# The seven half tiles of a mixture of experts spread among the whole ones, beside a linear recurrence

## The chip, the core and the metric

The kernel runs on one core of a Trainium2 chip. The metric is the device time of one execution in microseconds. The engines are TensorE (PE in the profile, PEld for its weight loads), VectorE (DVE), ScalarE (ACT), GpSimd (POOL) and SyncE (SP), which here only issues DMAs. All data is float32.

## The reference

Tokens x of shape (8, 512, 256) are normalised to xn. One branch is a recurrent attention with 16 heads of 16, the other a top-2 mixture of 8 experts (256 to 1024 to 256). The result is x + s * g.

```python
q, k = silu(x @ Wq), l2_norm(silu(x @ Wk)); v = x @ Wv
a = k * gamma[..., None] * exp(gk)
def step(S, inp):
    S = S * exp(gkt)[..., None]
    sab = einsum('bhk,bhkv->bhv', at, S)
    S = S + kt[..., None] * (sab[..., None, :] + vt[..., None, :])
    return S, einsum('bhk,bhkv->bhv', qt, S)
...
for e in range(num_experts):
    h = gelu(xf @ W1[e] + b1[e]); y = h @ W2[e] + b2[e]
    out = out + cw[:, e:e + 1] * y
...
xn = layernorm(x)
s = attn(xn); g = silu(layernorm(ffn(xn)) * gamma + beta)
return x + s * g
```

## The kernel before

**The recurrence.** The 512 steps are cut into 8 segments of 64, and these into chunks of 16 or 8 steps in turn (CS), 48 chunks in all. For each chunk there are two sets of small matmuls: `by_state` (L901), which multiplies the state, and `by_keys` (L966), which makes the addition to it. VectorE adds the values between the two (`add_v`, L932) and renews the state after them (`renew`, L978). This is a chain: each chunk needs the state of the one before. VectorE also solves each segment ahead of its chunks (`fine`, `solve`: L710 to L823) and works out its outputs after them (`output`, L1029, L1038). Each segment's data moves through DRAM in several steps, on the SP queue: raw (L657), fq (L787), kt (L823), R (L1009, L1012), the o store (L1042), KT for each chunk (L882) and the values vz (L871). `attend` then gates, normalises and projects a segment. For the last two segments its final part waits until the experts are done.

**The experts.** Rows are sorted by expert into blocks of 128. There are NXW = 32 whole tiles of two blocks and NXH = 7 half tiles of one, at numbers 32 to 38, which take the odd blocks of experts. Each tile is processed in the same way whatever expert it has:

- its two weights, 1 MB each, are loaded into one of two buffers each, on SP (`load_weights`, L1084 and L1086), always for every tile, and its rows are gathered on POOL (`load_rows`, L1072);
- `turn` transposes the rows (L1094, copied at L1098);
- the first layer (L1125) runs over the tile's 256 or 128 rows with 1024 columns, in four steps of two Gelus (L1133);
- the second layer (L1150) runs for each block of 128 rows, ScalarE scales the result (L1158), and an indirect DMA on POOL adds it to y_dram (`add_to_sums`, L1102).

Weights are asked for one tile ahead and rows two, both at the first of the four steps of a tile. Inside tiles there are also sixteen copies of 256 KB from x to out (L1139), one in every second tile, to which the results are added in the end.

**The order of the work.** Everything is written as generators that yield planned costs in units of about a microsecond: a step of the first layer is 1.9, a turn 0.9, a block of the second layer 3.9, so a whole tile 16.3 and a half tile 12.4. `stretch` walks the 48 chunks. Between the steps of a chunk it spends a share of the experts' remaining cost (`per_chunk`), so that about four chunks' worth (AFTER) is left behind the chain. Each engine then works in the order in which it got its instructions, but for a scheduler's small moves. After the last tile `fetch_sums` (L1282) reads y_dram back, and `finish` does the last norms, the product with the attention and the addition to out.

```python
beside_cost = experts_cost + (NTB - 2) * 7 * 1.8 + 16 * 0.8 + 8 * 8.6 + 10
...
per_chunk = max(0.0, beside_cost - beside.spent) / (chunks + AFTER)
```

Of the kernel before, what the change touches and what calls it, by code (L numbers as in the profile page):

```python
# [30 lines left out]
def recurrent_attn_moe_kernel(  # L31
# [29 lines left out]
    NF = DFF // P  # L61
    NTB = T // NB
# [6 lines left out]
    NXW, NXH = 2 * NT * P // TS, E - 1  # L69
    NX = NXW + NXH  # L70
# [8 lines left out]
    def bank(name):  # L79
        return ps_p.tile([P, 512], F32, tag="ps", name=name)  # L80
# [61 lines left out]
    for i in range(2):  # L142
        t = sp.tile([P, GC, 2 * D], F32, name=f"vz{i}", bufs=1)
# [5 lines left out]
    def rows_of(ap, s, bb):  # L149

        return ap.rearrange("(c bb) t d -> bb t c d", bb=2)[bb, s * NB : (s + 1) * NB]
# [913 lines left out]
    def pieces(t):  # L1065

        return range(2 * t, 2 * t + 2) if t < NXW else (NXW + t,)

    def load_rows(t):
        xs = cp[0].tile([P, TS // P, D], F32, name="xs", bufs=3)  # L1070
        for n, r in enumerate(pieces(t)):
            nc.gpsimd.indirect_dma_start(  # L1072
                out=xs[:, n],
                out_offset=None,
                in_=xn_dram[:, :],
                in_offset=bass.IndirectOffsetOnAxis(ap=source[:, r : r + 1], axis=0),
            )
        return xs

    def experts(mp):  # L1080
        def load_weights(t):
            e = nc.sync.value_load(owner[0:1, t : t + 1], min_val=0, max_val=E - 1)
            w1 = mp.tile([P, KD, DFF], F32, name="w1")
            nc.sync.dma_start(w1, W1[bass.ds(e, 1)].rearrange("o (j p) f -> p (o j) f", p=P))  # L1084
            w2 = mp.tile([P, NF, D], F32, name="w2")
            nc.sync.dma_start(w2, W2[bass.ds(e, 1)].rearrange("o (f p) d -> p (o f) d", p=P))  # L1086
            return w1, w2

        def turn(t, xs):
            size = len(pieces(t))  # L1090
            pt = bank("pt").rearrange("p (j t) -> p j t", j=KD)
            for j in range(KD):
                for n in range(size):
                    nc.tensor.transpose(  # L1094
                        pt[:, j, n * P : (n + 1) * P], xs[:, n, j * P : (j + 1) * P], ident
                    )
            xT = mp.tile([P, KD, TS], F32, name="xT_s")
            nc.scalar.copy(xT[:, :, : size * P], pt[:, :, : size * P])  # L1098
            return xT

        def add_to_sums(r, y):
            nc.gpsimd.indirect_dma_start(  # L1102
                out=y_dram[:, :],
                out_offset=bass.IndirectOffsetOnAxis(
                    ap=target[:, r : r + 1], axis=0
                ),
                in_=y,
                in_offset=None,
                compute_op=ALU.add,
            )  # L1110

        now_xs, nxt = now["rows"]
        w1, w2 = load_weights(0)
        xT = turn(0, now_xs)
        yield 0.9
        for t in range(NX):
            size = len(pieces(t)) * P
            hs = []
            for f in range(0, NF, 2):
                ph = bank("ph").rearrange("p (k t) -> p k t", k=2)  # L1120
                h = mp.tile([P, 2, TS], F32, name="h", bufs=6)
                hs.append(h)
                for k in range(2):
                    for j in range(KD):
                        nc.tensor.matmul(  # L1125
                            ph[:, k, :size],
                            w1[:, j, (f + k) * P : (f + k + 1) * P],
                            xT[:, j, :size],
                            start=(j == 0),
                            stop=(j == KD - 1),  # L1130
                        )
                for k in range(2):
                    nc.scalar.activation(  # L1133
                        h[:, k, :size], ph[:, k, :size], AF.Gelu, bias=bias[:, t, f + k : f + k + 1]
                    )
                if f == NF // 2 and t % 2 and t // 2 < 2 * NTB:

                    copy = t // 2 // 2, t // 2 % 2
                    nc.sync.dma_start(rows_of(out, *copy), rows_of(x, *copy))  # L1139
                if f == 0:  # L1140
                    now_xs, nxt = nxt, load_rows(t + 2) if t + 2 < NX else None
                    ahead = load_weights(t + 1) if t + 1 < NX else None
                yield 1.9
            if t + 1 < NX:
                xT = turn(t + 1, now_xs)
                yield 0.9
            for n, r in enumerate(pieces(t)):
                py = bank("py")[:, :D]
                for f in range(NF):
                    nc.tensor.matmul(  # L1150
                        py,
                        hs[f // 2][:, f % 2, n * P : (n + 1) * P],
                        w2[:, f],
                        start=(f == 0),
                        stop=(f == NF - 1),
                    )
                y = mp.tile([P, D], F32, name="y", bufs=4)
                nc.scalar.activation(y, py, AF.Identity, scale=weight[:, r : r + 1])  # L1158
                add_to_sums(r, y)
                if n == 0 and size == TS:  # L1160
                    yield 3.9
            if ahead:
                w1, w2 = ahead
            yield 3.9
# [209 lines left out]
    def everything_else():  # L1374

        for s in range(2, NTB):
            yield from project(s, xT_all[:, s])
        while not cp:
            yield WAIT
        projecting.close()  # L1380
        prologue.close()
        with tc.tile_pool(name="moe", bufs=2, side="right") as mp:
            yield from experts(mp)
        now["experts"] = True
        fp = late.enter_context(tc.tile_pool(name="fin", bufs=2, side="right"))
        for name, ap in (("gam", gamma), ("bet", beta)):
            now[name] = fp.tile([P, D], F32, name=f"{name}_sb", bufs=1)
            nc.sync.dma_start(now[name], ap.partition_broadcast(P))
        sums = [fetch_sums(fp, s) for s in range(NTB)]
        yield 1.0  # L1390
        for s in range(NTB):
            beside.queue.append(finish(fp, s, sums[s]))
# [134 lines left out]
```

## Time and profile before

| | us |
|---|---|
| median of 3 runs | 1149.81 |
| lowest, highest | 1142.53, 1151.08 |
| the profiled execution | 1155.78 |
| its span in the profile | 1154.1 |
| TensorE, matmuls of the first layer (L1125), busy | 291.5 |
| TensorE, matmuls of the second layer (L1150), busy | 274.2 |
| VectorE busy in the span | 883.9 |
| moved by DMA | 221.86 MB, 192 GB/s |
| of this, expert weights | 78 loads of 1 MB |

The mean granted clock of TensorE was 0.868. A row of a timeline has the start, the duration, the engine, the line, the operation, what is written and read, and in brackets the idle time of the engine ahead of it and what ended it. A row of a windows view has, for one stretch of the span, its length and the busy time of each engine in it, then the granted clock, the busy share of the DMA engines and their rate. Of a row on SPq the duration is that of the issue, not of the transfer.

### The profile page before, as it was taken

Reading aid. Unit: us, or ns where it says so; the run is one execution under the profiler, and the core shown is the slowest. Engines: PE = TensorE matmul, PEld = TensorE weight load, DVE = VectorE, ACT = ScalarE, POOL = GpSimd, SP = SyncE. Lnnn points to the kernel's source line nnn. Section 1 sums busy time; section 2 is a strip of 40 time slices with the busy share of each in tenths; the row PEclk is TensorE's granted clock in tenths of the full one; section 3 lists DMA queues with packets and bytes.
Section 4 is the critical chain, followed back from the end, with each engine's and each line's share of the span. In section 5 each row is a group of like instructions: output and inputs, shape, how many; then the busy total and the mean of one; then the engine's idle time right before and its main releaser. Section 6 shows DMA issues by size and latency. Waiting matters only on the chain. (4 is left out here: it accounts for less than half of the span.)

```text
span 1154.1 us, 24865 instructions
## 1 busy us (share of the span) xinstructions
PE 891.7 (77%) x9448; PEld 689.1 (60%) x9448; DVE 883.9 (77%) x1769; ACT 667.3 (58%) x1566; POOL 377.2 (33%) x312
## 2 busy tenths in 40 slices
PE   4979968528998799778979985898979789766600
PEld 2544544327786688566868764677758678665500
DVE  6579999959999985799979769999894282313194
ACT  2574546655467585656486773657665546443473
POOL 2300002102448433133553332456433243211334
PEclk9987988759999899788989987999979799878755
DMA  9676688697785979975796896767989876797468
GB/s 221 186 188 193 154 222 153 145 242 225 147 270 161 197 194 289 136 193 136 216 223 158 242 219 178 187 211 190 177 252 227 148 215 183 118 268 202 116 172 135
DMA packets 393254, 221.86 MB, mean 192 GB/s; under 512 B 280912, under 2 KB 362704, under 8 KB 392112
## 3 DMA queue, kind: packets, MB, share of 16 engines
q1 hardware_dynamic: 363248, 172.17, 60.5%
q0 software_dynamic: 25280, 43.93, 18.1%
q10 hardware_dynamic: 4608, 4.20, 1.4%
q8 instruction: 74, 1.21, 0.4%
q14 instruction: 44, 0.36, 0.1%
HBM read 152.07 MB, written 72.35 MB: 194 GB/s over the span
## 5 line engine op out<-in xcount | busy, mean ns | idle before, releaser
L1125 PE MATMUL ph<-xT_s,w 128*128 128x256 f32 (+1 forms) x1248 | 291.5, 393 | 23.1 <-DMA w<-in_L_ffn_W_dram 20.1
L1150 PE MATMUL py<-w,h 128*128 128x256 f32 x1136 | 274.2, 397 | 14.5 <-ACT h L1133 12.2
L1125 PEld LDWEIGHTS ph<-xT_s,w 128*128 128x128 f32 x1248 | 238.2, 209 | 61.5 <-issue 26.3
L1150 PEld LDWEIGHTS py<-w,h 128*128 128x128 f32 x1136 | 219.4, 198 | 49.7 <-ACT h L1133 14.9
L1102 POOL DMA_INDIRECT y_dram<-y,target x71 | 149.3, 2103 | 292.1 <-ACT y L1158 140.7
L911 ACT ACTIVATE sdec<-S,PcF 128x64 f32<-128x64 f32 x752 | 190.6, 341 | 85.6 <-DVE S L978 69.3
L1072 POOL DMA_INDIRECT xs<-xn_dram,source x71 | 128.4, 1808 | 316.5 <-PE pt L1094 139.3
L1133 ACT ACTIVATE h<-ph,bias 128x256 f32<-128x256 f32 (+1 forms) x312 | 121.7, 452 | 125.5 <-PE ph L1125 125.3
L978 DVE SCALAR_TENSOR_TENSOR S<-PC,heads,sdec 128x256 f32<-128x256 f32 x188 | 78.5, 476 | 58.8 <-PE PC L966 30.1
L966 PE MATMUL PC<-RO,KT 8*64 8x64 f32 (+1 forms) x3008 | 56.6, 249 | 48.6 <-DVE RO L932 37.3
L966 PEld LDWEIGHTS PC<-RO,KT 8*64 8x64 f32 (+1 forms) x3008 | 45.3, 145 | 71.9 <-DVE RO L932 45.0
L901 PE MATMUL PC<-S,FA 64*16 64x64 f32 (+1 forms) x3072 | 47.9, 235 | 50.2 <-DVE S L978 43.8
L1158 ACT ACTIVATE y<-py,weight 128x256 f32<-128x256 f32 x71 | 33.2, 468 | 82.7 <-PE py L1150 82.5
L901 PEld LDWEIGHTS PC<-S,FA 64*16 64x16 f32 (+1 forms) x3072 | 35.8, 101 | 67.4 <-DVE S L978 48.6
L736 DVE TENSOR_TENSOR scratch_q<-Z,X 128x64 f32<-128x64 f32 (+11 forms) x96 | 69.9, 728 | 0.0
L811 DVE TENSOR_TENSOR scratch_a<-Z,A 128x1020 f32<-128x1020 f32 (+21 forms) x88 | 67.0, 761 | 3.3 <-ACT fq L775 2.8
L749 DVE TENSOR_REDUCE Z<-scratch_q 128x4 f32<-128x64 f32 (+11 forms) x96 | 69.3, 722 | 0.0
L932 DVE TENSOR_TENSOR RO<-PC,vz 128x512 f32<-128x512 f32 x48 | 33.0, 687 | 45.8 <-PE PC L901 41.6
L819 DVE TENSOR_TENSOR Z<-Z,scratch_a 128x1020 f32<-128x1020 f32 (+21 forms) x88 | 66.9, 760 | 0.6
L753 DVE TENSOR_TENSOR Z<-Z,X 128x64 f32<-128x64 f32 (+10 forms) x88 | 60.0, 682 | 0.0
L736 DVE TENSOR_TENSOR scratch_a<-Z,X 128x64 f32<-128x64 f32 (+10 forms) x88 | 60.0, 681 | 0.0
L749 DVE TENSOR_REDUCE A<-scratch_a 128x4 f32<-128x64 f32 (+10 forms) x88 | 59.6, 677 | 0.0
(227 smaller groups left out, 1303.3 us busy)
## 6 DMA issues: line engine op xcount, KB each, us to landing
w<-in_L_ffn_W_dram SPq DMA_DIRECT2D x78, 1024.0 KB
kqd<-st_p SPq DMA_DIRECT2D x48, 256.0 KB
raw<-kqd SPq DMA_DIRECT2D x8, 1536.0 KB
fq<-fq SPq DMA_DIRECT2D x8, 1024.0 KB
xn_dram<-xn SPq DMA_DIRECT2D x8, 512.0 KB
v<-st_p ACTq DMA_DIRECT2D x32, 128.0 KB
y_dram<-st_b SPq DMA_DIRECT2D x16, 256.0 KB
out_dram<-in_L_attn_x_dram SPq DMA_DIRECT2D x16, 256.0 KB
```

Of the source, the lines that this page charges most:

```text
L736: nc.vector.tensor_tensor(pr, Z[:, :, :upto, C:], step[:, m, i].unsqueeze(2).to_broadcast([P, n, upto, HD]), ALU.mult,)
L749: now["work"] = nc.vector.tensor_reduce(to, pr, AX.X, ALU.add)
L811: nc.vector.tensor_tensor(pr, Z[:, :, l, l:].unsqueeze(2).to_broadcast([P, n, l, w]), A[:, :, l, :l].unsqueeze(3).to_broadcast([P, n, l, w ...
L901: nc.tensor.matmul(p1[32 * q : 32 * q + 2 * C, b, m], FA[lo : lo + SB, 4 * q + m, c], S[lo : lo + SB, q, m], start=True, stop=True,)
L911: nc.scalar.activation(dec[:, n // 4, n % 4], S[:, n // 4, n % 4], AF.Copy, scale=PcF[:, n, c : c + 1])
L966: nc.tensor.matmul(p4[b * SB : (b + 1) * SB, q, m], KT[32 * q : 32 * q + C, lo : lo + SB], ro[32 * q : 32 * q + C, lo : lo + SB], start=Tr ...
L978: nc.vector.scalar_tensor_tensor(S.rearrange(flat)[:, :, at], p4.rearrange(flat)[:, :, at], heads[:, h : h + 1], now["dec"].rearrange(flat ...
L1072: nc.gpsimd.indirect_dma_start(out=xs[:, n], out_offset=None, in_=xn_dram[:, :], in_offset=bass.IndirectOffsetOnAxis(ap=source[:, r : r + ...
L1102: nc.gpsimd.indirect_dma_start(out=y_dram[:, :], out_offset=bass.IndirectOffsetOnAxis(ap=target[:, r : r + 1], axis=0), in_=y, in_offset=None,
L1125: nc.tensor.matmul(ph[:, k, :size], w1[:, j, (f + k) * P : (f + k + 1) * P], xT[:, j, :size], start=(j == 0), stop=(j == KD - 1),)
L1133: nc.scalar.activation(h[:, k, :size], ph[:, k, :size], AF.Gelu, bias=bias[:, t, f + k : f + k + 1])
L1150: nc.tensor.matmul(py, hs[f // 2][:, f % 2, n * P : (n + 1) * P], w2[:, f], start=(f == 0), stop=(f == NF - 1),)
```

## The change

The tiles are no longer taken in the order of their numbers. A list `order` puts one half tile behind every fourth whole tile: 0, 1, 2, 3, 32, 4, 5, 6, 7, 33, and so on to 27, 38, and then 28 to 31. The loop walks positions `at` in this list. Loads of weights and gathers of rows go by the next positions, the copies of x to out go by the position and not by the tile's number. Which rows and which expert a tile has, the costs that it yields and the buffers stay as they were.

```diff
-        for t in range(NX):
+
+        order, each = [], NXW // (NXH + 1)
+        for t in range(NXW):
+            order.append(t)
+            if t % each == each - 1 and t // each < NXH:
+                order.append(NXW + t // each)
+        for at, t in enumerate(order):
             size = len(pieces(t)) * P
...
-                if f == NF // 2 and t % 2 and t // 2 < 2 * NTB:
-
-                    copy = t // 2 // 2, t // 2 % 2
+                if f == NF // 2 and at % 2 and at // 2 < 2 * NTB:
+
+                    copy = at // 2 // 2, at // 2 % 2
                     nc.sync.dma_start(rows_of(out, *copy), rows_of(x, *copy))
                 if f == 0:
-                    now_xs, nxt = nxt, load_rows(t + 2) if t + 2 < NX else None
-                    ahead = load_weights(t + 1) if t + 1 < NX else None
+                    now_xs, nxt = nxt, load_rows(order[at + 2]) if at + 2 < NX else None
+                    ahead = load_weights(order[at + 1]) if at + 1 < NX else None
                 yield 1.9
-            if t + 1 < NX:
-                xT = turn(t + 1, now_xs)
+            if at + 1 < NX:
+                xT = turn(order[at + 1], now_xs)
                 yield 0.9
```

## The prediction

> **What bounds the kernel now.** I read the page first, then the windows view cut at places of the state chain, then TensorE's timeline behind the chain, then the timeline of the SP queue around one change of segment.
>
> ```profile
> span 1154.1 us, 24865 instructions
> ...
> PE 891.7 (77%) x9448; PEld 689.1 (60%) x9448; DVE 883.9 (77%) x1769; ACT 667.3 (58%) x1566; POOL 377.2 (33%) x312
> ...
> DVE  6579999959999985799979769999894282313194
> ...
> DMA  9676688697785979975796896767989876797468
> ```
>
> No engine is full over the span, but VectorE (DVE) is at nine tenths through most of slices 9 to 31, then falls to two or three: its work belongs to the recurrence. The DMA engines are never idle.
>
> ```profile
> core 0: us, PE busy (x) PEld busy (x) DVE busy (x) ACT busy (x) POOL busy (x), PEclk, DMA share, GB/s
> 254.80:882.20 627.40, 540.64 (x6523) 443.51 (x6523) 554.66 (x964) 404.59 (x1022) 262.49 (x173) 0.91 0.84 202
> 882.20:1010.80 128.60, 109.81 (x1523) 91.60 (x1522) 61.00 (x144) 63.53 (x195) 42.45 (x34) 0.90 0.77 166
> 1010.80:1081.10 70.30, 49.35 (x267) 42.93 (x265) 16.42 (x55) 31.47 (x71) 9.87 (x9) 0.82 0.74 191
> 1081.10:1154.10 73.00, 8.07 (x42) 6.90 (x40) 41.96 (x106) 32.54 (x56) 32.61 (x35) 0.57 0.74 164
> ```
>
> The cuts are the 5th, the 40th and the end of the 48th state product (L901), and the last scatter of the experts (L1102). In the first 627 us TensorE is busy 86% and VectorE 88%: two engines that hand work to each other, both nearly full. In the next 129 us VectorE is at 47% and TensorE at 85%. Then come 70 us in which the chain is over and TensorE has experts alone, and 73 us of final norms, which start only after the last scatter.
>
> ```profile
> 1015.63 5.78 PE L1125 MATMUL ph<-xT_s,w 128*128 128x128 f32 x32 [4.78 <-DMA w<-in_L_ffn_W_dram]
> ...
> 1025.74 3.73 PE L1125 MATMUL ph<-xT_s,w 128*128 128x128 f32 x32
> ...
> 1044.50 3.72 PE L1150 MATMUL py<-w,h 128*128 128x256 f32 x16 [0.46 <-ACT h L1133]
> 1054.19 5.44 PE L1125 MATMUL ph<-xT_s,w 128*128 128x128 f32 x32 [5.97 <-DMA w<-in_L_ffn_W_dram]
> ...
> 1067.48 5.44 PE L1125 MATMUL ph<-xT_s,w 128*128 128x128 f32 x32 [2.64 <-DMA w<-in_L_ffn_W_dram]
> ```
>
> This is the tail of half tiles. The work of one is 3.73 + 0.38 + 3.7 = 7.8 us, yet the first shown starts at 1015.63 and the fourth after it at 1067.48: 13.0 us each. In the brackets is the wait: the weights. After a wait the same 32 matmuls take 5.4 to 5.8 us in place of 3.73.
>
> **The change part by part.** No instruction is added or taken away: 39 tiles, 71 scatters, 78 weight loads of 1 MB stay. Three things move: the order of the tiles, with their loads on SP and gathers on POOL; the sixteen copies of x to out, which count positions now; and, since the planner pays 12.4 units for a half and 16.3 for a whole, which tiles lie behind the chain. A whole is 2 x 3.72 + 0.6 + 7.07 = 15.1 us of TensorE at full clock (timeline rows), a half 7.8.
>
> From the two programs' orders of instructions on TensorE I count the work in each window, 7.44 us for a whole first layer, 3.73 for a half one, 3.54 for one second-layer block of 128 rows:
> - Up to the 40th product: before 28 wholes and 55 blocks, after 24 wholes, 5 halves and 53 blocks: 403.0 becomes 384.8, -18.2 us.
> - 40th to 48th: before 4 wholes, 2 halves, 11 blocks (76.2), after 5, 2 and 10 (80.1): +3.9 us.
> - Behind the chain: before 5 halves, 5 blocks (36.4), after 3 wholes, 8 blocks (50.6): +14.2 us.
>
> *First window.* The 18 us are real for TensorE, but VectorE binds as much: in a stretch such as 334 to 363 it has no idle time at all. Only the segments of 16 steps have TensorE as the fuller (429 to 459: 29.7 of 30.0 us against 18.7), and two of the first five halves stand there. A third of the 18 us: -6, bounds -18 and 0. Against it stand the weights. A pair is issued at the first group of the tile ahead of its use. A row for the empty-queue case: the last half's loads are issued at 1059.75 and 1060.38, its matmuls are released at 1067.48, so 7.7 us for the first megabyte. Under a whole tile there are 13 to 23 us between issue and use (658.02 to 670.91, 397.75 to 420.71), and the two waits in this window sum to 3.1 us. Behind a half there are 7.3 us less. Where that hurts is seen on the SP queue:
>
> ```profile
> 658.02 0.40 SPq L1084 DMA_DIRECT2D w<-in_L_ffn_W_dram  x1
> ...
> 663.80 3.32 SPq L657 DMA_DIRECT2D raw<-kqd  x1
> 667.37 0.38 SPq L1086 DMA_DIRECT2D w<-in_L_ffn_W_dram  x1
> ...
> 673.39 10.91 SPq L1042 DMA_DIRECT2D o<-O  x1
> 687.14 6.39 SPq L882 DMA_DIRECT2D KT<-kt  x8
> 693.64 1.35 SPq L871 DMA_DIRECT2D vz<-v  x4
> 696.11 0.41 SPq L1084 DMA_DIRECT2D w<-in_L_ffn_W_dram  x1
> ```
>
> At a change of segment the second half of a pair is held 9 us behind raw and its like, and the next pair follows a store of VectorE's output that holds the queue for 10.91 us. The second and the fourth half stand just before such a change. What is queued behind a weight wait on TensorE is the next state or key product, and VectorE's update waits for that. I take 3 us at two halves outside the changes, nothing at one, and 3 us at each of the two at a change: with the lower clock after a wait some +12, less 3 that a half's lighter TensorE load hides: +9. Bounds: 0 (all hidden) and +38 (5 halves x 7.7 us: the 5.97 us wait at 1054 and the 1.7 us of slow clock after it).
>
> Here a rule speaks against the change. The row: 13.0 us for a half with its pair, in the tail. The Trainium skill, page "DMA: Bandwidth & Descriptors", section "Bandwidth", has 6.15 us for a load of one megabyte alone (on GpSimd's queue), so 12.3 us for a pair as an estimate: a half's 7.8 us could never cover the next one. Seven times 4.5 us would be +31 us of stall, and the sum below about +22 instead of near nothing. I don't take it, since in the chain a half doesn't last 7.8 us: a product interval of about 15 us takes 12.8 planned units, so a half is spread over some 14 us with products in between.
>
> *40th to 48th.* Behind the 44th product the changed program has 40.0 us of expert work where it had 29.1 (2.5 wholes' first layers, one half, 5 blocks against 1, 2 and 4). TensorE idled 8.8 us there, of which a 3.27 us wait for KT and a 3.26 us wait for VectorE now have matmuls ahead of them: +11 - 6 = +5. Ahead of the 44th product 7 us go, but there the SP queue and the output of the segment before bind: -1. Together +4, bounds -3 and +11.
>
> *Behind the chain.* 50.6 us plus 1.8 of transposes and 1.1 of L1225 is 53.5, and weights fit under wholes: -15 if TensorE alone counted. But ScalarE must do the last segment's sigmoid (L1229) before the last tile's Gelus, and that waits for R, the output and its reload. Before, the sigmoid comes at 1064.73, 53.9 us after the chain, and 16.4 us later is the last scatter. R's loads stand on SP behind one more weight pair, which waits for a tile two before; that wait now ends after a block pair, 7 us after the chain, and R starts about 8 us after it, not 19. So the sigmoid about 43 to 46 us after the chain, and 60 to 62 us in all: -9. Since ScalarE works in program order, one late R gives it all back: bounds -15 and 0. I take -8.
>
> *Copies and gathers.* The copies come one or two products earlier, from a region with 0.77 DMA share into one with 0.84: the last eight are 4 MB of traffic; nothing, hidden by slack before the final accumulation; if not, one 256 KB copy delays a KT by about 1 us. Gathers are two tiles ahead still, on POOL at 33%: nothing. The 73 us of norms don't change.
>
> Sum: -6 + 9 + 4 - 8 = -1 us. The sum stands against the profiled execution, 1155.78 us with a span of 1154.1; the median of the three runs shown is 6 us lower, so I forecast 1149 us.
>
> **The rivals.** (a) *The weights bind in the chain*, slower. Mechanism: a pair behind a half is stuck on SP behind raw, fq and the o store, TensorE stops at L1125, the products queue behind it. Price: 5 to 6 halves at 5 to 7 us, +33, less the tail's 8 and 6 of the lighter load, plus 4: +23, 1173 us. It decides from a mean stall of some 4 us for a half. For it: DMA share 1.0 in the 16-step segments; against it: only 3.1 us of weight waits in 627 us now. (b) *TensorE is the real limit in the first window*, faster: -15 of the 18 us count, stalls are +4, then +4, then -13 in the tail: -20, 1130 us. For it: 540.6 of 627 us busy and rows without gaps from 412 to 459; against it: VectorE full in the 8-step segments, which are most. (c) *The tail doesn't shrink* because the attention's last segment binds it (R late): -6 + 9 + 4 = +7, 1157 us, still within a per cent. That the halves are not where the change puts them is excluded by the order of instructions.
>
> **How the numbers follow.** One per cent, about what a measurement of this kernel can tell, is 11.5 us: below 1138.3 and above 1161.3. Forecast and (c) together 0.5, (a) 0.29, (b) 0.21. A twentieth of the forecast's case ends on each side, mostly the slow one: faster 0.23, same 0.45, slower 0.32. The range goes from 1134, inside (b), to 1174, the price of (a).
>
> **What would show it.** Right: the stretch from the 48th product to the last scatter near 61 us, with no weight wait in it; the 5th to the 40th product within 8 us of 627; weight waits of TensorE ahead of the 40th product 6 to 15 us in sum, each in a tile after a half. Wrong by (a): over 25 us of such waits, and a longer first window. Wrong by (b): a first window under 615 us. The tail's step is wrong if the sigmoid still comes over 52 us after the chain.

## The result, and the profile after

| | before | changed |
|---|---|---|
| median, us | 1150.44 (4 runs, 1142.53 to 1151.93) | 1163.56 (4 runs, 1156.81 to 1166.99) |
| ratio | | 1.0138, 95% interval 1.0091 to 1.0185 |

The change makes the kernel 1.4% slower, 13.1 us between the medians, where -1 us was forecast. The profiled execution of the changed kernel took 1156.81 us, the fastest of its four; that of the kernel before took 1155.78 us, more than any of the four runs in the table. So the two profiles differ by 1 us only. They show where time moved, but not the size of the loss. A second profile of the changed kernel (c1 in the table further on, 1160.92 us) has the same places. The page of the first:

```profile
span 1155.1 us, 24864 instructions
...
PE 884.0 (77%) x9448; PEld 684.8 (59%) x9448; DVE 882.3 (76%) x1769; ACT 664.7 (58%) x1563; POOL 392.9 (34%) x312
...
DVE  7579999959999975999949759999894554323194
```

Busy times say little: they are nearly those of before. The windows view says more, cut at the same places as before (5th, 40th and end of the 48th state product, last scatter):

```profile
251.30:899.50 648.20, 527.96 (x6512) 436.36 (x6512) 558.38 (x969) 398.66 (x1026) 262.92 (x166) 0.90 0.85 199
899.50:1023.80 124.30, 112.34 (x1548) 93.84 (x1548) 57.10 (x141) 67.12 (x201) 50.77 (x38) 0.93 0.82 197
1023.80:1083.00 59.20, 56.59 (x272) 48.41 (x273) 15.06 (x54) 32.64 (x61) 15.03 (x12) 1.00 0.65 143
1083.00:1155.10 72.10, 3.73 (x18) 2.94 (x16) 41.94 (x106) 30.95 (x52) 32.56 (x35) 0.55 0.75 166
```

The stretch behind the chain fell from 70.3 to 59.2 us, the one before it from 128.6 to 124.3. The 5th product comes 3.5 us sooner. Only the first window grew: 627.4 to 648.2 us. There TensorE is busy 12.7 us less, where 18 were counted, and VectorE (the third pair of numbers) 3.7 us more. VectorE's idle time, length less busy time, went from 72.7 to 89.8 us. Busy and idle time make up the length for any engine, so this alone does not tell which one holds the others up. The waits tell more. TensorE's wait for VectorE's renewal of the state, ahead of the next state product, grew by 15 us (before and then after; us in total, times, longest):

```profile
PE PC L901 <- DVE S L978: 31.6, 9, 12.3
```

```profile
PE PC L901 <- DVE S L978: 46.8, 12, 13.6
```

Behind the chain TensorE's timeline has no weight wait any more, and the granted clock is 1.00:

```profile
1030.69 7.07 PE L1131 MATMUL ph<-xT_s,w 128*128 128x256 f32 x32
...
1046.21 7.07 PE L1131 MATMUL ph<-xT_s,w 128*128 128x256 f32 x32
...
1054.27 7.17 PE L1156 MATMUL py<-w,h 128*128 128x256 f32 x32 [0.55 <-ACT h L1139]
1061.28 3.62 PE L1131 MATMUL ph<-xT_s,w 128*128 128x256 f32 x16
1066.95 3.72 PE L1131 MATMUL ph<-xT_s,w 128*128 128x256 f32 x16 [2.06 <-ACT attn L1235]
```

What VectorE waited for in the first window, before and then after, from the waits view (us in total, times, longest):

```profile
DVE RO L932 <- PE PC L901: 18.5, 5, 7.0
DVE S L978 <- PE PC L966: 18.2, 5, 7.6
DVE dec L716 <- ACT X L669: 14.7, 3, 6.9
...
DVE scratch_a L811 <- ACT fq L775: 2.0, 3, 0.8
```

```profile
DVE S L978 <- PE PC L966: 25.3, 5, 7.8
DVE dec L716 <- ACT X L669: 22.0, 4, 11.2
DVE RO L932 <- PE PC L901: 10.2, 3, 6.6
DVE scratch_a L811 <- ACT fq L775: 8.7, 4, 3.9
```

The longest single wait is new: 11.2 us for X, ScalarE's copies of raw (L669), at the change to the sixth segment. Followed back through the queues of the changed kernel, VectorE, ScalarE, SP and POOL in turn:

```profile
595.78 0.23 DVE L716 COPY dec<-X 128x128 f32<-128x128 f32 x1 [11.24 <-ACT X L669]
```

```profile
577.67 0.47 ACT L1164 ACTIVATE y<-py,weight 128x256 f32<-128x256 f32 x1 [1.67 <-PE py L1156]
592.00 5.58 ACT L669 COPY X<-raw 128x1024 f32<-128x1024 f32 x3 [13.86 <-DMA raw<-kqd]
```

```profile
552.54 0.39 SPq L1086 DMA_DIRECT2D w<-in_L_ffn_W_dram  x1
573.64 0.80 SPq L1205 DMA_DIRECT2D attn<-og  x2
...
581.15 3.04 SPq L657 DMA_DIRECT2D raw<-kqd  x1
...
594.19 0.41 SPq L1084 DMA_DIRECT2D w<-in_L_ffn_W_dram  x1
```

```profile
544.93 5.20 POOL L1072 DMA_INDIRECT xs<-xn_dram,source  x1 [10.95 <-PE pt L1094]
550.43 7.85 POOL L1072 DMA_INDIRECT xs<-xn_dram,source  x1 [0.30 <-issue]
558.58 1.63 POOL L1102 DMA_INDIRECT y_dram<-y,target  x1 [0.30 <-ACT h L1139]
564.57 4.64 POOL L1102 DMA_INDIRECT y_dram<-y,target  x1 [4.36 <-ACT xT_s L1098]
568.66 1.42 POOL L1282 DMA_DIRECT2D att<-attn  x1
```

Read from below. The attention of an earlier segment is done with its buffer when POOL has stored it (L1282); ScalarE wrote its last part at 554.33. But ahead of that store POOL has two gathers, 5.20 and 7.85 us long, and two scatters, so it comes at 568.66. In SP's queue the next attention's first request (L1205) needs that buffer, and SP issues nothing from 552.9 to 573.64. Behind it stands raw, which ScalarE needs, and ScalarE stands still for 13.86 us ahead of its copies. VectorE waits for them, and behind its wait stands the chain's own addition (L932): TensorE's product for it was issued to the end at 589.0, the addition comes at 600.88. In the kernel before the same requests are issued 14 us sooner, and neither ScalarE's copies nor VectorE's L716 have idle time ahead of them:

```profile
558.96 1.33 SPq L1199 DMA_DIRECT2D attn<-og  x2
...
566.79 3.11 SPq L657 DMA_DIRECT2D raw<-kqd  x1
...
578.84 0.41 SPq L1084 DMA_DIRECT2D w<-in_L_ffn_W_dram  x1
```

```profile
580.99 5.76 ACT L669 COPY X<-raw 128x1024 f32<-128x1024 f32 x3
```

```profile
590.67 0.22 DVE L716 COPY dec<-X 128x128 f32<-128x128 f32 x1
```

The weight pair behind raw was held as well, and TensorE then waited for it, though under a whole tile, the second behind a half:

```profile
599.64 10.10 PE L1131 MATMUL ph<-xT_s,w 128*128 128x256 f32 x32 [10.64 <-DMA w<-in_L_ffn_W_dram]
```

### The profile page after: what moved, and what is told of

Read it like the earlier page. It is cut to its first block, busy times and chain, and to the rows that moved or that the text cites. A ratio compares the mean times of both kernels' runs of the same rounds, so it can differ in the third digit from the quotient of the medians.

```text
span 1155.1 us, 24864 instructions
## 1 busy us (share of the span) xinstructions
PE 884.0 (77%) x9448; PEld 684.8 (59%) x9448; DVE 882.3 (76%) x1769; ACT 664.7 (58%) x1563; POOL 392.9 (34%) x312
## 3 DMA queue, kind: packets, MB, share of 16 engines
q0 software_dynamic: 25280, 43.93, 17.8%
## 4 chain that ended last, share of the span: by engine, by line
DVE 38%; PE 30%; DMA 11%; ACT 8%; issue 7%; SPq 3%; POOL 1%; ACTq 0%; POOLq 0%; DVEq 0%
PE ph L1131 10%; PE py L1156 9%; DVE scratch_q L736 5%; DVE Z L753 4%; DVE Z L749 4%; DVE A L749 4%; DVE S L978 3%; DVE scratch_a L736 3%; ACT sdec L911 2%; PE po L1261 2%; PE PC L966 2%; ACT X L669 2%; PE pp L261 2%; DVE scratch_a L811 2%; DVE scratch_o L1029 2%
## 5 line engine op out<-in xcount | busy, mean ns | idle before, releaser
L1156 PE MATMUL py<-w,h 128*128 128x256 f32 x1136 | 265.3, 389 | 15.4 <-ACT h L1139 13.0
L1072 POOL DMA_INDIRECT xs<-xn_dram,source x71 | 144.9, 2040 | 322.3 <-PE pt L1094 150.6
L1156 PEld LDWEIGHTS py<-w,h 128*128 128x128 f32 x1136 | 215.2, 194 | 49.0 <-ACT h L1139 15.5
L932 DVE TENSOR_TENSOR RO<-PC,vz 128x512 f32<-128x512 f32 x48 | 32.9, 684 | 41.7 <-PE PC L901 23.8
L669 ACT COPY X<-raw 128x1024 f32<-128x1024 f32 x24 | 45.8, 1974 | 27.7 <-DMA raw<-kqd 27.7
## 6 DMA issues: line engine op xcount, KB each, us to landing
v<-st_p ACTq DMA_DIRECT2D x32, 128.0 KB
```

The source lines that it names most:

```text
L1072: nc.gpsimd.indirect_dma_start(out=xs[:, n], out_offset=None, in_=xn_dram[:, :], in_offset=bass.IndirectOffsetOnAxis(ap=source[:, r : r + ...
L1156: nc.tensor.matmul(py, hs[f // 2][:, f % 2, n * P : (n + 1) * P], w2[:, f], start=(f == 0), stop=(f == NF - 1),)
```

## The experiments

The theories, with the short names that some expectations use: the halves' own weight pairs bind in the chain (T1); what matters is where the stream of tiles stands against the changes of segment (T2); the plan's price of a half, 12.4 for some 8 us, spoils the mixture; any pair of weights costs its transfer, whoever it belongs to (T4); SP is held by the attention's requests (T5). All runs in one table; ratios are to the kernel before on the same chip. The stretches and VectorE's idle time are from each run's profile, worked out as above. "Raw" is the time of the request for the sixth segment's raw, and ScalarE's idle time ahead of its copies.

| run | ratio (95%) | 5th to 40th | to end of 48th | tail | VectorE idle | raw, wait |
|---|---|---|---|---|---|---|
| before | 1 | 627.4 | 128.7 | 70.5 | 72.8 | 567, 0 |
| changed | 1.0138 | 648.2 | 124.2 | 59.2 | 89.9 | 581, 13.9 |
| c1 | 1.0162 (1.0099 to 1.0225) | 649.8 | 121.2 | 62.7 | 91.1 | 582, 14.1 |
| e1 | 0.9965 (0.9944 to 0.9985) | 623.3 | 135.0 | 54.4 | 69.0 | 568, 0 |
| e2 | 0.9958 (0.9937 to 0.9979) | 633.1 | 124.9 | 55.5 | 72.6 | 575, 18.4 |
| e3 | 1.0099 (1.0076 to 1.0121) | 636.7 | 128.1 | 58.2 | 78.6 | 568, 0 |
| e4 | 1.0085 (1.0062 to 1.0108) | 638.3 | 127.8 | 62.6 | 81.0 | 563, 0 |
| e5 | 0.9800 (0.9722 to 0.9879) | 613.3 | 123.2 | 69.0 | 57.8 | 552, 2.3 |
| e6 | 1.0071 (1.0049 to 1.0094) | 610.2 | 128.9 | 65.2 | 77.6 | 580, 0 |
| e7 | 1.0102 (1.0036 to 1.0168) | 623.2 | 122.4 | 61.9 | 85.4 | 577, 4.0 |
| e8 | 1.0095 (1.0067 to 1.0124) | 621.8 | 132.8 | 60.8 | 71.0 | 550, 0 |
| e9 | 0.9795 (0.9737 to 0.9854) | 592.3 | 123.8 | 53.0 | 46.4 | 550, 5.2 |
| e10 | 1.0282 (1.0223 to 1.0341) | 651.3 | 134.4 | 55.6 | 96.5 | 583, 12.0 |
| e11 | 1.0162 (1.0100 to 1.0223) | 627.9 | 135.3 | 64.4 | 75.1 | 582, 10.4 |
| e12 | 0.9995 (0.9976 to 1.0013) | 626.6 | 125.0 | 66.8 | 71.4 | 551, 0 |
| e13 | 0.9989 (0.9969 to 1.0008) | 637.0 | 118.9 | 63.5 | 77.6 | 561, 0 |
| e14 | 0.9792 (0.9729 to 0.9856) | 600.9 | 130.5 | 52.3 | 44.9 | 549, 0 |
| e15 | 0.9844 (0.9796 to 0.9892) | 594.1 | 127.1 | 55.4 | 48.6 | 545, 6.5 |
| e16 | 0.9951 (0.9924 to 0.9978) | 623.7 | 135.3 | 59.0 | 60.4 | 543, 0 |
| e17 | 0.9642 (0.9563 to 0.9722) | 610.7 | 128.0 | 53.0 | 51.5 | 532, 0 |

e6 and e7 do some 20 us of VectorE's work ahead of the 5th product, so their first windows compare only with each other. Each row has one profile, taken on one of several chips, while the row "before" has the profile of 1155.78 us named above: e8's profile is 2 us shorter than it, though e8's runs are 0.95% slower than those of the kernel before on their chip. So a few us between two rows can be those of the execution. The totals in the expectations were set against some 1150 us; on the chips of these runs the kernel before took 1140.7 to 1150.4 us, so it is the ratios that tell.

A cut at one product is loose as well, since a product's place among the matmuls of the tiles shifts. The same profiles by product: how much later than in the kernel before a state product starts, counted from the 5th (a minus is sooner), and how long TensorE waited for weights between the 5th and the 40th, in us (before: 3.1).

| run | raw | 22nd | 31st | 38th | 40th | 41st | TensorE's waits for weights |
|---|---|---|---|---|---|---|---|
| changed | late | -2.1 | 13.9 | 17.8 | 20.8 | 18.4 | 18.5 |
| c1 | late | -2.8 | 13.3 | 18.9 | 22.4 | 21.2 | 13.2 |
| e2 | late | -10.2 | 2.7 | 2.0 | 5.7 | 2.7 | 7.7 |
| e10 | late | 3.2 | 19.9 | 26.0 | 23.9 | 30.5 | 0.7 |
| e11 | late | -3.3 | 17.4 | 18.7 | 0.5 | 15.0 | 0.0 |
| e3 | in time | -2.8 | 4.3 | 8.3 | 9.3 | 6.8 | 13.8 |
| e4 | in time | -0.5 | 4.2 | 12.9 | 10.9 | 10.3 | 28.4 |
| e12 | in time | 2.3 | 0.7 | 1.0 | -0.8 | -1.2 | 7.1 |
| e13 | in time | -0.1 | 2.6 | 8.4 | 9.6 | 7.1 | 24.5 |

Between the 22nd and the 31st product, where raw of the sixth segment is needed, the five runs with it late lose 12.9 to 20.7 us, the three of the changed order with it in time 2.7 to 7.1, and e12, the old order, nothing. TensorE's waits for weights do not go with the loss: e10 and e11 hardly have any and are among the slowest, and e4 and e13 have the most.

**Where the halves stand: e1, e11, e10, and c1.**

```diff
# e1: the seven halves in a row, ahead of the last four whole tiles
...
+        order = [*range(NXW - 4), *range(NXW, NX), *range(NXW - 4, NXW)]
# e10: behind tiles 1, 5, ... 25
-            if t % each == each - 1 and t // each < NXH:
+            if t % each == 1 and t // each < NXH:
# e11: the third and the fifth half moved to just ahead of the last
+        for t in (NXW + 2, NXW + 4):
+            order.remove(t)
+            order.insert(order.index(NXW + 6), t)
```

> Order 0 to 27, the seven halves, 28 to 31: the halves stand where VectorE has little to do, and whole tiles still form the tail. Theory T1 (the halves' weight pairs disturb the chain wherever VectorE is full, so the loss is in the first window, to the 40th product): the first window is back near 627 us, the tail stays near 55, total 1135 to 1143, faster than before. Theory T2 (the loss is an accident of the order on the POOL and SP queues): anything, first window between 620 and 650. Theory T3 (the loss comes with having halves in the chain at all, also in the last segment): the 40th to 48th window grows from 124 to over 145 us, total 1150 or more.

> One half behind every fourth whole tile still, but behind tiles 1, 5, 9 to 25 in place of 3, 7 to 27, so that they meet the changes of segment elsewhere. T5: the two jumps move or go, first window anything from 622 to 645 us and not at the same products. T1: the same loss of 15 to 22 us, spread or at new places, first window 640 to 652.

> The changed order, but the two halves ahead of the two jumps (the third and the fifth, behind tiles 11 and 19) are moved to stand just ahead of the last half; three halves stay in the first window. T5: both jumps go, first window within 5 us of 627, tail under 62 us, total 1136 to 1146, at or under before. T1 (each half costs about 4 us): first window 636 to 642.

> The changed kernel once more, for runs and a trace on the same chip as the next three: a ratio of 1.009 to 1.018, the first window (5th to 40th product) 640 to 650 us, the tail under 60 us. If the first window of this second trace is under 632 us, the loss of 21 us seen in the first trace was one execution's, and the reasons built on it fall.

c1 is the changed kernel once more: the loss repeats, at the same places (its tail, 62.7 us, is over the 60 that were forecast). With no half in the first 28 tiles (e1) the first window is that of before and the tail is still short, 54.4 us: the tail's gain doesn't need halves in the chain. e1 is 0.35% faster than before. Shifting the halves by two tiles (e10) makes the loss 2.8%. Taking two of the five out (e11) seems to save 20 us in the first window, but that is the cut: its 40th product is 0.5 us late, while the 38th is 18.7 and the 41st 15.0 us late, about as in the changed kernel, and its loss is that of the changed kernel too. Raw is held in e11 although the third half no longer stands ahead of it. Both runs have raw at 582 to 583, and e11 meets neither forecast.

**Pairs of weights: e2 and e5.** e2 leaves out the halves' own weights (a half uses those of the tile before it); e5 leaves out those of five whole tiles in the old order.

```diff
# e2
-                    ahead = load_weights(order[at + 1]) if at + 1 < NX else None
+                    ahead = None
+                    if at + 1 < NX and order[at + 1] < NXW:
+                        ahead = load_weights(order[at + 1])
# e5
...
+                    if t + 1 < NX and t + 1 not in (4, 9, 14, 19, 24):
+                        ahead = load_weights(t + 1)
```

> The changed order, but a half tile loads no weights of its own and uses those of the tile before it: 14 MB of loads less, the rest unchanged. This leaves out the right weights of the half tiles. T1: first window from 648 to 630 us or less, total 1140 or less. T2: the first window stays within 5 us of 648, since the SP queue is still held by the store of the attention, total over 1150.

> The old order, but five whole tiles of the first window (4, 9, 14, 19, 24) load no weights and use those of the tile before; this leaves out their right weights. It asks whether taking five pairs away is worth 15 us in any order, as it was in the changed one, or only where the pairs belong to half tiles. T1 (halves' pairs are the trouble): the first window stays within 5 us of 627, total at most 5 us below before. T4 (every pair of weights costs the first window about 3 us, whoever it belongs to): first window 612 us, total about 15 us below before.

Without the halves' pairs the first window is 15 to 17 us shorter, though raw is still held; neither forecast for the window (630 or less, or within 5 us of 648) is met. But five pairs taken from whole tiles of the old order are worth 14.1 us too. So by these two runs a pair in this window costs about 3 us whoever it belongs to, and e2 shows no price that is special to a half: T1 is not what sets the two orders apart, which load 28 and 29 pairs there.

**The held request: e3 and e4.** e3 puts POOL's store of the attention on ScalarE's queue; e4 tells the plan that a step of a half is 0.95.

```diff
# e3
-        nc.gpsimd.dma_start(att_d[s].rearrange("n p d -> p n d"), o)
+        nc.scalar.dma_start(att_d[s].rearrange("n p d -> p n d"), o)
# e4
-                yield 1.9
+                yield 1.9 if size == TS else 0.95
...
-    ... + NXH * (4 * 1.9 + 0.9 + 3.9)
+    ... + NXH * (4 * 0.95 + 0.9 + 3.9)
```

> The changed order, with the store of a segment's attention (L1282 in the changed kernel) issued from ScalarE's queue, right behind the copy that makes it, in place of POOL's. T2: SP's waits at L1205 for that store fall from 27.4 us to under 8, first window down by 10 to 20 us, total 1145 to 1153. T1: SP's waits fall too, but the first window moves less than 5 us, total 1158 to 1165.

> The changed order, with a half tile's four first-layer steps planned at 0.95 in place of 1.9 (8.6 units in place of 12.4), so that chunks with a half get as much TensorE work as others and less is left for later. If the planner's price causes the loss (18 us of work pushed out of the first window while the chain waits): total 1145 to 1153, the first window not longer than 648. T1: halves pass faster, the time between pairs shrinks, first window 650 to 665, total 1165 or more.

SP and ScalarE of e3, at the same place:

```profile
560.33 0.80 SPq L1205 DMA_DIRECT2D attn<-og  x2
...
568.08 2.81 SPq L657 DMA_DIRECT2D raw<-kqd  x1
```

```profile
580.27 5.75 ACT L669 COPY X<-raw 128x1024 f32<-128x1024 f32 x3
```

The store no longer stands behind gathers, raw is requested 13 us sooner, ScalarE doesn't wait, and the first window is 636.7 us: 11.5 less than the changed kernel, 13.1 less than c1. In e4 raw comes at 563 and the window is 638.3. Both leave about 10 us over the old order. e3 meets the forecast for a held request (10 to 20 us off the window). But in all it wins only 0.4 to 0.6% of the 1.4 to 1.6%: its next stretch is 128.1 us, where it was 124.2 and 121.2, and takes part of the gain back.

**The phase: e6, e7, e12, e13.** EARLY is the share of the experts ahead of the first chunk, 110 in both kernels. Lower or higher, it shifts the whole stream of tiles.

```diff
-EARLY = 110.0
+EARLY = 102.0    # e6 old order, e7 changed order
+EARLY = 118.0    # e12 old order, e13 changed order
```

> The old order with EARLY at 102 in place of 110: the experts start half a chunk later against the chain, nothing else. T2 (the loss is that of any new interleaving against an order that was tuned): the first window grows by 6 to 20 us, total 1.005 to 1.015. T1: it grows less than 5 us, total within 0.3% but for the shift itself.

> The changed order with EARLY at 102. T2: the changed order finds another interleaving, its first window moves by 8 us or more either way, so that its ratio to before moves out of 1.009 to 1.018. T1: the loss stays, ratio 1.009 to 1.02, first window 638 to 655.

> The old order with the share of experts ahead of the first chunk raised from 110 to 118 units. If the place of the tiles against the changes of segment is the cause, the old order loses here too, as it did with 102: 1.005 to 1.015 of the time before. If the halves are the cause, the old order stays within 0.995 to 1.005.

> The changed order with the same shift. If the halves cost whatever the phase, this is 1 to 1.5% above the run of the old order with the same shift. If it is the place, the two lie within 0.5% of each other, or the changed order is ahead.

The changed order costs 1.4 to 1.6% at 110 and nothing at 118. At 102 it costs some 0.3% against e6, which the intervals do not tell from nothing, and e6 itself is 0.7% slower than the kernel before. e12 keeps to what was forecast if the halves are the cause, e13 to what was forecast if the place is: neither reading holds alone. SP and ScalarE of e13:

```profile
561.30 3.19 SPq L657 DMA_DIRECT2D raw<-kqd  x1
...
571.14 1.12 SPq L1205 DMA_DIRECT2D attn<-og  x2
```

```profile
581.02 5.84 ACT L669 COPY X<-raw 128x1024 f32<-128x1024 f32 x3
```

Here the attention's request stands behind raw, not ahead of it, so its wait for the store holds nothing that ScalarE needs. The first window is 637.0 us against 626.6 of e12, 10.4 more; the two later stretches give back 6.1 and 3.3, and the two kernels take the same time.

**The attention's requests on POOL: e8, e9, e14 to e17.** The three loads of `attend` go to POOL's queue instead of SP's. e8 has the changed order, e9 the old one; e14 is e8 with e4's price; e15 is e1's order; e16 and e17 are e8 and e9 with EARLY at 118.

```diff
-            nc.sync.dma_start(og1[lo : lo + HD], og_d[s])
+            nc.gpsimd.dma_start(og1[lo : lo + HD], og_d[s])
...
-                nc.sync.dma_start(
+                nc.gpsimd.dma_start(
...
-            nc.sync.dma_start(
+            nc.gpsimd.dma_start(
```

> The changed order, with the attention's loads (og, ro and o) issued on POOL in place of SP, so that a weight pair never stands behind their wait for the store of the segment before. T5 (the first window's loss is two collisions, at the 24th to 25th and at the 36th product, in which the pair of the second whole tile behind a half stands on SP behind those loads): both jumps against before go, first window 622 to 634 us, SP's wait for that store gone, total 1136 to 1146. T1 (a half leaves its successor too little lead anywhere): the jumps stay, first window over 640.

> The old order with the same move of the attention's loads, as the control of the run before. T5: the old order hardly has the collision, so it gains little: first window 618 to 630 us, tail still near 70, total 1138 to 1150. If it gains as much as the changed order does (15 us or more), the move is a gain of its own and says nothing of the change.

> The changed order with the attention's three loads on POOL and a half's first-layer step priced at 0.95. If the price is half of the loss, 0.75 to 1% less than the changed order with the loads on POOL alone had (1.0095), so near 1.001. If the price matters only where SP was held by the attention, no difference: 1.007 to 1.012.

> All seven halves just ahead of the last four whole tiles, and the attention's three loads on POOL. If the two gains add up (0.9965 of the halves, 0.9795 of the loads): 0.976, near 1115 us. If the tail's gain was already in the loads' move (its tail was 53 us where the changed order has 59): 0.980, no better than the loads alone.

> The changed order, the attention's three loads on POOL, 118 units ahead of the first chunk. If the 1.0095 of the same kernel with 110 units was the place at which its tiles stood, this falls to 0.98 to 0.99. If it was the halves themselves, 1.005 to 1.012 again.

> The old order with the same two edits. If the loads' move gains 2% by itself, 0.975 to 0.985 as with 110 units. If that gain was a lucky place too, 0.99 to 1.005.

If SP being held had been the whole cause, e8 would have matched e9. It doesn't: 621.8 against 592.3 us in the first window, 3% in all, and about 3% again between e16 and e17. So T5 alone does not explain the loss. And e9, the control, gains 2.1%: the move of the loads is a gain of its own. In e8 raw is in time, but the wait has moved to VectorE, which shows in its timeline, first e8 and then e14, which has the same tiles beside this chunk:

```profile
596.89 0.68 DVE L932 TENSOR_TENSOR RO<-PC,vz 128x512 f32<-128x512 f32 x1
612.17 1.23 DVE L1224 TENSOR_TENSOR attn<-attn 128x1024 f32<-128x1024 f32 x1 [14.60 <-DMA attn<-o]
...
616.97 1.65 DVE L978 SCALAR_TENSOR_TENSOR S<-PC,heads,sdec 128x256 f32<-128x256 f32 x4
```

```profile
595.74 0.69 DVE L932 TENSOR_TENSOR RO<-PC,vz 128x512 f32<-128x512 f32 x1
...
600.00 1.66 DVE L978 SCALAR_TENSOR_TENSOR S<-PC,heads,sdec 128x256 f32<-128x256 f32 x4
604.05 1.23 DVE L1224 TENSOR_TENSOR attn<-attn 128x1024 f32<-128x1024 f32 x1 [2.39 <-DMA attn<-o]
```

In e8 the attention's addition (L1224), which waits for its own load, got its place ahead of the renewal of the state. The chain stands for 14.60 us: e8's 25th product is 3.5 us ahead of e14's, its 26th 13.5 us behind. At 835.56 the same addition waits once more, for 11.77 us, which a scatter on POOL's queue ended. With a half's step priced at 0.95 the renewal is ahead, and e14 takes no more than e9 (0.9792 and 0.9795). In e16 the same addition waits for 6.5 us there; what the rest of its 3% is wasn't found. e15 doesn't add e1's gain to e9's: its tail is 55.4 us, and that of e9 was already 53.0. e14, e16 and e17 lie outside both ranges that were forecast for them. The best kernel of the study is e17, the old order with the loads moved and EARLY at 118: 1109.54 us, 3.6% under the kernel before; e9, without the shift, took 1116.28 us.

## Why the prediction failed

*Behind the chain* was right: 60 to 62 us forecast, 59.2 measured (62.7 in c1), no weight wait, and by the way that was forecast. R's loads come 7.6 us after the chain, where 8 was forecast, and the last sigmoid (L1235) at 1066.3, 42.5 us after it, where 43 to 46 was:

```profile
1031.37 11.72 SPq L1012 DMA_DIRECT2D R<-ro  x16
```

(70.3 less TensorE's 53.5 us is 16.8 and not the 15 of the prediction, but the forecast didn't rest on it.)

*40th to 48th*: +4 forecast, -4.4 measured (-7.5 in c1), just outside the lower bound of -3; cut at the 41st product it is -2.0 (-6.3). Work moved in (TensorE's busy time rose from 109.8 to 112.3 us), but it filled idle time; no more than that was looked into.

*First window* is the step that failed: +3 forecast, +20.8 measured. It was the sum of two terms.

- "A third of the 18 us: -6" was wrong. TensorE's relief was 12.7 us of busy time, and no gain shows for it. The two stretches named as TensorE's, each with a half in it now, did not get shorter: 30.0 us became 30.8 (15th to 17th product), 31.0 became 32.7 (27th to 29th). At the 24th product, with three of the five halves done, the changed kernel is level with the one before (0.2 us sooner).
- "+9" for TensorE's weight waits has the size of the waits, and that is luck. TensorE has 18.5 us of them in this window (13.2 in c1) against 3.1. But the two long ones (10.64 and 5.60 us) are not in a tile right after a half. They are in the second whole tile behind one; at the first of them SP came late, as shown above. And the loss does not follow them: e10 loses 24 us in this window with 0.7 us of such waits, and e11 is 18.7 us late at the 38th product with none.
- The missing term is raw, held in SP's queue behind a request that waited for a POOL store. It is worth 10 to 13 us of the first window, and 9 to 11 between the 22nd and the 31st product (e3 and e4 against the changed kernel and c1). e3 is the test of it, since it moves the store and nothing else; e4 and e13 agree, but move the tiles too. The prediction had seen SP's queue at changes of segment, had read in it only what delays the weights, and had put the gathers on POOL, at 33%, at nothing. What ScalarE needs from SP's queue was not looked at.

So of the 20.8 us some 10 to 13 are the late raw, which had no term, and the -6 did not come. The rest, 9 to 11 us, is left in e3, e4 and e13 and stays open. Part of it lies between the 31st and the 38th product, where the fifth half stands: 4 to 9 us in the changed kernel, c1, e3, e4 and e13, but 1.3 in e11, which has that half elsewhere, and -0.7 in e2, where it loads no weights. That points at its pair, but it was not tested alone.

Rival (a) named the right queue and window, with the wrong thing held in it: its price came from TensorE's stalls, which stayed under its mark of 25 us. Rival (b) is refuted by the longer first window, rival (c) by the shorter tail. The rule weighed in the prediction, with 12.3 us for a pair as an estimate from the Trainium skill's page "DMA: Bandwidth & Descriptors", section "Bandwidth", would have given +22, closer to the measured +13 than -1 is. But its reason, 31 us of stalls behind halves, is not what happened.

What stays open besides: why halves among the whole tiles lead to these orders of requests. The plan's price is part of it, and the phase another, but neither alone. With the attention's loads on POOL the price removes the loss (e14 against e9) and the phase doesn't (e16 against e17); with them on SP the phase removes it (e13) and the price only part of it (e4).

## What to carry to other kernels

When work beside a chain is moved, don't only ask whether its own loads come in time: look at each in-order queue at the places where the chain changes data, and list which request may wait there (for a buffer, for another queue's store) and what stands behind it. A change of order is best tried at two or three phases of the stream: here the same change costs 1.5% at one, nothing at the next. And keep a request that can wait off the queue that feeds the chain, and the operation that uses it behind the chain's own.

## What was not expected of the hardware

Two gathers on POOL that took 2.56 and 0.99 us in the kernel before (531.66, 534.52) took 5.20 and 7.85 us in the changed one (5.48 and 7.84 in c1), and why is not shown. Spans on POOL are rough, but the store behind them was late, and SP's wait for it, 20.6 us, is not a matter of spans. And five weight pairs less, 10 MB of 222, made the old order 2% faster (e5), although TensorE waited only 3.1 us for weights in the window where they were taken out. So pairs cost this chain more than the waits that show. Whether that is their traffic or their place in SP's queue (raw is requested 15 us sooner in e5) was not separated.
